# Where layer 0 adds its output bias: VectorE on the residual, or GpSimd on the gathered x

## The chip, the cores and the metric

The kernel runs on one core of one Trainium2 chip. The metric is the device time of one execution in microseconds (us), the median of several runs. One further execution was recorded by the hardware profiler; all lines of a profile come from that one.

## The reference, cut to what matters

Two transformer layers over a graph of 2708 tokens of width 512, 8 heads of 64. A token attends only to its neighbours. The layers have the same form:

```
q, k, v  = h @ Wq.T + bq,  h @ Wk.T + bk,  h @ Wv.T + bv
scores   = q . k / 8, and -1e9 where adj and the diagonal are both 0
ctx      = softmax(scores) @ v
h1 = layer_norm(h + ctx @ Wo.T + bo) * ln1_g + ln1_b
h2 = layer_norm(h1 + relu(h1 @ W1.T + b1) @ W2.T + b2) * ln2_g + ln2_b
```

In layer 0, `h` is the input `x`. The sum `h + ctx @ Wo.T + bo` is what the change touches: three terms, added in one order or in another. Everything is float32.

## The kernel before, in words

**Order of the tokens.** The kernel first finds the neighbours of every token and sorts the tokens by how many they have. Rank by rank they fall into 22 tiles of 128 tokens (the last has 20). A token's row of `x` is therefore fetched by an indirect DMA with the indices `ident_i`; this is the `gather` helper, line 982, which GpSimd issues. Keys and values of the neighbours (`kv`) come the same way, one gather for each neighbour slot of a tile.

**Attention, a step at a time.** `attend` is a generator. One step takes up to two neighbour slots of a tile: VectorE multiplies `kv` by `q` (L1019) and reduces (L1025), ScalarE takes the exponentials `p` (L1038) and weighs half of the values (L1045), VectorE weighs the other half (L1051) and adds them up in `acc` (L1058). When a tile is through, ScalarE divides (`cx`, L1089). There are five `kv` buffers, and a gather into one waits until `acc` has been added from it.

**Blocks.** The dense work goes in 11 blocks of two tiles. For each block, `attended` turns `cx` with TensorE (`tp`, L1128), gathers the tile's rows of `x` into `xb` (layer 0), and yields; then, tile by tile, it projects with Wo (`o`, L569), adds `xb` (`h`, L1254), in layer 0 adds the bias row `bo` (L1256), and normalises. `norm` is six instructions: statistics (L1112), their aggregate (L1114), `va` (L1116) on VectorE, then `rd`, a power on GpSimd (L1118), and two multiply-adds on VectorE (L1119 beside `rd`, L1122 after it). `turned` flips `h` with TensorE into `hT` (L1128, L1133). `feed_forward` then runs 16 steps `f` of eight matmuls `pf` (L1296), one ScalarE `ft` (L1304) and matmuls into `a` (L1284), and at its end adds `a` and `h` (L1316) and normalises again.

**Staging.** In the 16 steps of block k, `attended` of block k+1 starts at f = 10 and its projections come at f = 11 (one step later for k = 0). Between the steps, `advance` runs attention steps for coming tiles, paced by a credit.

**Who sets the order.** TensorE, ScalarE and the SP queue run in the order in which the program is written. VectorE and GpSimd are ordered by the compiler's planner, except inside `manual_schedule`: during the first stage and the first queries GpSimd runs as written, during the first queries VectorE too, and GpSimd runs as written through block 0 of layer 0 (`in_order`). That covers `attended` of blocks 0 and 1. From block 1's own steps on, the planner places GpSimd's instructions. An `xb` buffer comes from a ring of three (tag `row`); the planner issues the gather into it as soon as it is free.

Of the kernel before, what the change touches and what calls it, by code (L numbers as in the profile page):

```python
# [13 lines left out]
ALU = mybir.AluOpType  # L14
# [457 lines left out]
def by_edges(ctx: ExitStack, tc: tile.TileContext, x, xT, adj, layers, out, good):  # L472
# [9 lines left out]
    nc = tc.nc  # L482
# [82 lines left out]
    def project(xs, r, wm, name, other=False):  # L565

        o = (ps_f if other else ps).tile([P, DM], F32, tag="f" if other else "g", name=name)
        for c in range(NC):
            nc.tensor.matmul(o[:r], xs(c), wm[:, c, :], start=(c == 0), stop=(c == NC - 1))  # L569
        return o  # L570
# [10 lines left out]
    def size(g):  # L581
        return min(P, N - g * P)
# [390 lines left out]
    def fetch(n, to, table, g):  # L973

        r = size(g)
        if n == 0:
            gather(to[:r], table, ident_i[:r, g : g + 1])
        else:
            nc.sync.dma_start(out=to[:r], in_=table[g * P : g * P + r, :])
# [129 lines left out]
    def norm(z, r, gain, shift):  # L1109

        st = small.tile([P, 6], F32, tag="st", name="st")
        nc.vector.bn_stats(st[:r], z[:r])  # L1112
        mv = small.tile([P, 2], F32, tag="mv", name="mv")
        nc.vector.bn_aggr(mv[:r], st[:r])  # L1114
        va = small.tile([P, 1], F32, tag="va", name="va")
        nc.vector.tensor_scalar(va[:r], mv[:r, 1:2], EPS, None, ALU.add)  # L1116
        rd = small.tile([P, 1], F32, tag="rd", name="rd")
        nc.gpsimd.tensor_tensor(rd[:r], va[:r], mhalf[:r], ALU.pow)  # L1118
        nc.vector.scalar_tensor_tensor(  # L1119
            z[:r], z[:r], mv[:r, 0:1], gain[:r], ALU.subtract, ALU.mult  # L1120
        )
        nc.vector.scalar_tensor_tensor(z[:r], z[:r], rd[:r], shift[:r], ALU.mult, ALU.add)  # L1122

    def flip(z, r, to, shift=None):

        tp = ps.tile([P, NC, P], F32, tag="g", name="tp")
        for c in range(NC):
            nc.tensor.transpose(tp[:, c, :r], z[:r, c * P : (c + 1) * P], ident[:r, :r])  # L1128
        if shift is None:
            nc.scalar.copy(to, tp[:, :, :r])  # L1130
            return
        for c in range(NC):
            nc.scalar.activation(  # L1133
                to[:, c, :], tp[:, c, :r], AF.Identity, bias=shift[:, c : c + 1]
            )

    class Layer:
# [101 lines left out]
        def attended(self, block, got):  # L1239

            cTs, hs = [], []
            for g in block:
                r = size(g)
                cx = got.pop(g)
                cT = dn.tile([P, NC, P], F32, tag="cT", name="cT", bufs=3)
                flip(cx, r, cT[:, :, :r], self.bv)
                xb = dn.tile([P, DM], F32, tag="row", name="xb", bufs=3)
                fetch(self.n, xb, x if self.n == 0 else xb_d[self.n], g)
                cTs.append((g, r, cT, xb))
            yield  # L1250
            for g, r, cT, xb in cTs:
                o = project(lambda c: cT[:, c, :r], r, self.wo, "o")
                h = dn.tile([P, DM], F32, tag="h", name="h", bufs=4)
                nc.vector.tensor_tensor(h[:r], o[:r], xb[:r], ALU.add)  # L1254
                if self.n == 0:
                    nc.vector.tensor_tensor(h[:r], h[:r], self.bo[:r], ALU.add)  # L1256
                norm(h, r, self.g1, self.e1b2)
                hs.append(h)
                yield
            yield hs  # L1260
# [383 lines left out]
```

## Time and profile before

| what | value |
|---|---|
| median of 3 runs | 1964.92 us (1962.63 to 1966.28) |
| profiled execution, its own time | 1964.63 us |
| its span, first to last instruction | 1962.9 us |
| TensorE busy | 1901.0 us |
| VectorE busy | 1300.8 us |
| ScalarE busy | 933.8 us |
| GpSimd busy | 796.8 us |
| mean granted TensorE clock | 0.989 |

In the lines of the profile PE is TensorE's matmuls, PEld its weight loads, DVE VectorE, ACT ScalarE, POOL GpSimd and SP SyncE. L12 is line 12 of the kernel. A group or a line is written as output<-inputs by the program's names. A wait line gives who waited for whom, the total in us, how many times and the longest; a timeline line gives start, duration, engine, line and operation, and in brackets the idle time just before it and what ended it.

### The profile page before, as it was taken

The page shows a single profiled execution, that of the slowest core. Times are in us where ns is not written, and L with a number is a line of the kernel's source. Part 1 is how long each engine was busy: PE and PEld are TensorE (multiplying, and loading weights), DVE is VectorE, ACT ScalarE, POOL GpSimd, SP SyncE. Part 2 cuts the span into 40 slices and gives each one's busy share as a digit, 9 for nine tenths or more (in the row PEclk, how much of TensorE's full clock was granted, in tenths as well). Part 3 has the DMA queues.
Part 4 walks back from the last instruction along what each step waited for, and adds up shares of the span by engine and source line. Part 5 has one row for each costly group of instructions (what it writes and reads, how often), then busy time and mean ns, then how long its engine had stood idle before and what let it go on. Part 6 is the DMA issues. An engine that isn't in the chain of part 4 may idle for free. (4 is left out here: it accounts for less than half of the span.)

```text
span 1962.9 us, 20872 instructions
## 1 busy us (share of the span) xinstructions
PE 1901.0 (97%) x6162; PEld 1100.6 (56%) x6162; DVE 1300.8 (66%) x2142; ACT 933.8 (48%) x3219; POOL 796.8 (41%) x710
## 2 busy tenths in 40 slices
PE   8999988999999999999999998999999999999997
PEld 4444444565565655566556643556666566666664
DVE  5884587685867869659442036888688988877421
ACT  4660254564555655547332112756456765755410
POOL 3114635453555535425310022555347655644210
PEclk9999999999999999999999999999999999999998
DMA  9998766455655556546310646856455766554000
GB/s 327 352 311 307 258 211 235 161 166 189 202 161 199 188 186 227 161 150 204 130 43 27 230 162 215 298 174 217 153 177 198 247 214 209 186 190 154 34 11 13
DMA packets 131486, 366.92 MB, mean 187 GB/s; under 512 B 16668, under 2 KB 36988, under 8 KB 128654
## 3 DMA queue, kind: packets, MB, share of 16 engines
q0 software_dynamic: 69120, 246.35, 37.9%
q1 hardware_dynamic: 53332, 99.66, 14.9%
q10 hardware_dynamic: 8910, 19.48, 2.6%
q8 instruction: 50, 0.82, 0.2%
q14 instruction: 74, 0.61, 0.1%
HBM read 314.62 MB, written 50.83 MB: 186 GB/s over the span
## 5 line engine op out<-in xcount | busy, mean ns | idle before, releaser
L982 POOL DMA_INDIRECT kv<-kv_d,idx x420 | 546.1, 1300 | 475.9 <-DVE acc L1058 319.1
L1284 PE MATMUL a<-w,ft 128*128 128x512 f32 (+1 forms) x1408 | 669.9, 601 | 10.8 <-ACT ft L1304 9.5
L1296 PE MATMUL pf<-hT,w 128*128 128x256 f32 (+1 forms) x2816 | 636.3, 373 | 13.2 <-ACT ft L1304 8.8
L1296 PEld LDWEIGHTS pf<-hT,w 128*128 128x128 f32 x2816 | 521.1, 191 | 192.2 <-issue 107.3
L1284 PEld LDWEIGHTS a<-w,ft 128*128 128x128 f32 (+1 forms) x1408 | 256.5, 187 | 239.0 <-issue 201.4
L1304 ACT ACTIVATE ft<-pf,b 128x256 f32<-128x256 f32 (+1 forms) x352 | 158.5, 459 | 424.8 <-PE pf L1296 424.5
L1019 DVE TENSOR_TENSOR kv<-kv,q 128x1024 f32<-128x1024 f32 (+3 forms) x222 | 256.5, 1158 | 156.3 <-DMA kv<-kv_d,idx 103.7
L1045 ACT ACTIVATE kv<-kv,p 128x64 f32<-128x64 f32 x1232 | 311.0, 335 | 5.0
L1025 DVE TENSOR_REDUCE sc<-kv 128x16 f32<-128x1024 f32 (+3 forms) x222 | 255.2, 1154 | 1.4
L1058 DVE TENSOR_TENSOR acc<-acc,kv 128x1024 f32<-128x1024 f32 (+2 forms) x178 | 204.0, 1146 | 26.7 <-ACT kv L1045 25.9
L1118 POOL TENSOR_TENSOR rd<-va,mhalf 128x1 f32<-128x1 f32 (+1 forms) x88 | 85.4, 971 | 267.6 <-DVE va L1116 266.2
L1038 ACT ACTIVATE p<-sc,minus 128x8 f32<-128x8 f32 (+1 forms) x420 | 103.4, 295 | 161.1 <-DVE sc L1025 154.6
L569 PE MATMUL o<-wo,cT 128*128 128x512 f32 (+1 forms) x352 | 157.8, 601 | 3.7 <-DVE qs L1226 3.3
L1051 DVE TENSOR_TENSOR kv<-kv,p 128x512 f32<-128x512 f32 (+1 forms) x178 | 121.6, 684 | 52.8 <-ACT p L1038 52.7
L569 PEld LDWEIGHTS o<-wo,cT 128*128 128x128 f32 (+1 forms) x352 | 65.5, 187 | 92.2 <-issue 80.9
L1089 ACT ACTIVATE cx<-acc,su 128x64 f32<-128x64 f32 (+1 forms) x352 | 88.4, 333 | 42.6 <-DVE su L1081 33.9
L1316 DVE TENSOR_TENSOR h<-a,h 128x512 f32<-128x512 f32 (+1 forms) x44 | 29.7, 677 | 106.8 <-PE a L1284 106.7
L1122 DVE SCALAR_TENSOR_TENSOR h<-h,rd,ln_b 128x512 f32<-128x512 f32 (+1 forms) x88 | 65.9, 749 | 50.9 <-POOL rd L1118 50.9
L663 ACT ACTIVATE code<-aj 128x2708 bf16<-128x2708 int32 (+1 forms) x22 | 73.2, 3329 | 49.1 <-POOL aj L659 45.4
L1355 POOL DMA_INDIRECT kv_d<-kvs,ident_i x22 | 23.7, 1077 | 179.0 <-ACT kvs L1349 110.9
L666 DVE MAX8 tops<-code 128x8 f32<-128x247 f32 (+2 forms) x242 | 83.1, 400 | 19.3 <-ACT code L663 19.3
L1045 ACT ACTIVATE acc<-kv,p 128x64 f32<-128x64 f32 (+1 forms) x352 | 88.8, 334 | 1.4
(133 smaller groups left out, 1514.2 us busy)
## 6 DMA issues: line engine op xcount, KB each, us to landing
aj<-in_adj SPq DMA_DIRECT2D x21, 1354.0 KB, 8.0
kv_d<-kvs ACTq DMA_DIRECT2D x21, 512.0 KB, 5.6
w<-in_W SPq DMA_DIRECT2D x20, 512.0 KB, 4.8
xg<-in_xT SPq DMA_DIRECT2D x19, 512.0 KB, 8.8
kv<-kv_d,idx POOLq DMA_INDIRECT x420, 5.6
w<-in_W ACTq DMA_DIRECT2D x12, 512.0 KB, 8.9
q_d<-qs SPq DMA_DIRECT2D x22, 256.0 KB, 4.2
zT_d<-zT SPq DMA_DIRECT2D x22, 256.0 KB, 5.3
```

What stands on the lines that cost most here:

```text
L569: nc.tensor.matmul(o[:r], xs(c), wm[:, c, :], start=(c == 0), stop=(c == NC - 1))
L982: nc.gpsimd.indirect_dma_start(out=to, out_offset=None, in_=table[:, :], in_offset=bass.IndirectOffsetOnAxis(ap=s, axis=0), bounds_check=N ...
L1019: nc.vector.tensor_tensor(kv[:r, :c, :DM], kv[:r, :c, :DM], self.q[:r].unsqueeze(1).to_broadcast([r, c, DM]), ALU.mult,)
L1025: nc.vector.tensor_reduce(self.sc[:r, s0 : s0 + c, :], kv[:r, :c, :DM].rearrange("p s (h d) -> p s h d", d=DK), AX.X, ALU.add,)
L1038: nc.scalar.activation(p[:r, s, :], self.sc[:r, s, :], AF.Exp, bias=minus[:r, g, s : s + 1])
L1045: nc.scalar.activation(to[:, i, hd], kv[:r, i, DM + h * DK : DM + (h + 1) * DK], AF.Copy, scale=p[:r, s0 + i, h : h + 1],)
L1051: nc.vector.tensor_tensor(to[:, 0, :].rearrange("p (h d) -> p h d", d=DK), kv[:r, 0, DM:].rearrange("p (h d) -> p h d", d=DK), p[:r, s0, : ...
L1058: nc.vector.tensor_tensor(self.acc[:r, :c, :], self.acc[:r, :c, :], kv[:r, :c, DM:], ALU.add)
L1089: nc.scalar.activation(cx[:r, hd], self.acc[:r, 0, hd], AF.Copy, scale=self.su[:r, h : h + 1])
L1284: nc.tensor.matmul(a[:r], fts[f][:, c0 : c0 + r], self.w2[f // 2][:, f % 2, :], start=(f == 0), stop=(f == NFC - 1),)
L1296: nc.tensor.matmul(pf[:, :w], self.w1[f // 2][:, c, f % 2 * P : f % 2 * P + P], hT[:, c, :w], start=(c == 0), stop=(c == NC - 1),)
L1304: nc.scalar.activation(ft[:, :w], pf[:, :w], AF.Relu, bias=self.b1[:, f : f + 1])
```

## The change

In layer 0, the bias row `bo` is added to the gathered `xb` by GpSimd, for both tiles of the block after the `yield`, ahead of the projections. The addition to `h` on VectorE goes. Layer 1 has no such addition and stays as written.

```diff
             yield
+            if self.n == 0:
+                for g, r, cT, xb in cTs:
+                    nc.gpsimd.tensor_tensor(xb[:r], xb[:r], self.bo[:r], ALU.add)
             for g, r, cT, xb in cTs:
                 o = project(lambda c: cT[:, c, :r], r, self.wo, "o")
                 h = dn.tile([P, DM], F32, tag="h", name="h", bufs=4)
                 nc.vector.tensor_tensor(h[:r], o[:r], xb[:r], ALU.add)
-                if self.n == 0:
-                    nc.vector.tensor_tensor(h[:r], h[:r], self.bo[:r], ALU.add)
                 norm(h, r, self.g1, self.e1b2)
```

## The prediction

> **What bounds the kernel now.** I read the page's busy times first.
>
> ```profile
> PE 1901.0 (97%) x6162; PEld 1100.6 (56%) x6162; DVE 1300.8 (66%) x2142; ACT 933.8 (48%) x3219; POOL 796.8 (41%) x710
> ```
>
> TensorE leaves 1962.9 - 1901.0 = 62 us. No edit on VectorE or GpSimd can gain more than the part of those idle times that it shortens, and it loses where it adds to them. Next I asked who makes TensorE wait in layer 0's dense part (264 to 1060 us): some 20 us in all, most of it in three places. These lines are from TensorE's waits in 264 to 300, 300 to 345 and 625 to 665 us:
>
> ```profile
> PE pf L1296 <- ACT ft L1304: 7.6, 3, 3.5
> ...
> PE tp L1128 <- DVE h L1122: 3.9, 1, 3.9
> ...
> PE tp L1128 <- ACT cx L1089: 3.8, 1, 3.8
> ```
>
> Only the second is a wait for the chain that the change shortens: block 1's `h` (329.26 to 333.12 us). The other two are attention that comes late. A wait costs more than itself; busy times by stretch show the clock (10 us each, PEclk is the third number from the end):
>
> ```profile
> 329.00:339.00 10.00, 6.14 (x14) 1.61 (x12) 6.54 (x12) 2.81 (x11) 6.91 (x6) 0.66 0.49 148
> 339.00:349.00 10.00, 10.00 (x40) 7.50 (x41) 8.71 (x16) 4.21 (x17) 4.70 (x5) 1.00 0.65 232
> ```
>
> 0.66 is 6.8 us at half clock and 3.2 us at full. The half clock overlaps the wait itself, so what it takes from matmuls is some 2.5 us. The same 0.66 stands at 274 to 284 and at 632 to 642 us.
>
> **What the Trainium skill says.** "TensorE: Matmul & The Clock Gate", Part 1: an idle window of about 3.4 us halves the clock, which comes back after about as much work. The trace agrees: waits of 2.8 to 3.9 us were each followed by the half clock, waits up to 2.3 us in layer 0's later blocks by none. "SBUF — State Buffer", SBUF: two separate sides: GpSimd shares a port pair with VectorE, as an exclusive lock; a VectorE instruction with two SBUF inputs and a GpSimd instruction that reads SBUF do not overlap. The trace fits: `rd`, one column on GpSimd, takes 0.58 us at the least and 2.06 us at the most, long where VectorE runs such instructions (1.60 us at 330.68). Price of the new add: "GPSIMD Engine Reference", Elementwise, gives about 2.6 cycles an element at 1.2 GHz, so my estimate for 512 elements is 1.1 us and start-up. The nearest row:
>
> ```profile
> L659 POOL TENSOR_TENSOR aj<-aj,diag 128x128 int32<-128x128 int32 (+1 forms) x22 | 9.7, 442 | 78.6 <-DMA aj<-in_adj 74.7 <-ACT kvs L863 3.8
> ```
>
> Four times its 0.44 us is 1.8 us. I take 1.2 us, with 1.1 and 1.8 as ends, and up to 1.2 us more behind a VectorE instruction that holds the ports (L1058 runs 1.2 us).
>
> **The change, part by part.**
>
> Removed from VectorE, by the query for this line:
>
> ```profile
> L1256 DVE TENSOR_TENSOR h<-h,bo x22: 678/686/693, 256.3 to 1050.6; 128x512 f32<-128x512 f32 x21, 20x512 f32<-20x512 f32 x1
> ```
>
> 22 x 0.686 = 15.1 us busy; back to back they start 0.6 to 0.7 us apart, so about 14 us of time. Against it the lock: 22 adds x 1.2 us = 26 us in which VectorE's two-input instructions wait. At about half the time in such instructions that takes back some 13 us. VectorE as a whole gains nothing (between -14 and +12 us), under a TensorE that is the bound.
>
> Added to GpSimd: 22 adds, 26 us of 1963, no DMA. The 22 `xb` gathers stay. The wait for their landing (2.9 to 6.7 us after issue, median 4.5) moves from VectorE's `h` to GpSimd's add; queued behind that add are the gathers of `kv` and `q`, `rd`, and the writes of `kv_d`. VectorE's `h` now waits for GpSimd. What that does depends on the block.
>
> *Block 0*, all in written order. GpSimd's timeline:
>
> ```profile
> 245.31 0.99 POOL L982 DMA_INDIRECT kv<-kv_d,idx  x1 [0.30 <-issue]
> 258.19 1.02 POOL L1118 TENSOR_TENSOR rd<-va,mhalf 20x1 f32<-20x1 f32 x1 [11.89 <-DVE va L1116]
> ```
>
> Both adds fit into the 11.89 us of idle time: `xb` was issued by 240.5 and has landed by 246, the adds end by about 249 us, and `h` starts at 255.62. VectorE's norm chain up to 264.24 loses 2 x 0.71 = 1.4 us. TensorE does not wait for it (its own queries last until 263.9), but the attention behind it on VectorE does start 1.4 us sooner, and that feeds the 7.6 us of waits for `ft`. ScalarE stands between: `p` at 267.33 is written behind an `ft` that TensorE releases at 266.82, so it gains only 0.2 to 0.3 us there unless the planner reorders. I take -0.4 us, ends -1.4 and 0.
>
> *Block 1*, GpSimd still in written order, VectorE by the planner. By the program the adds (f = 12) stand behind the attention steps that f = 11 paid for, four `kv` gathers, and ahead of `rd`:
>
> ```profile
> 305.40 1.00 POOL L982 DMA_INDIRECT xb<-in_x,ident_i  x1 [0.31 <-issue]
> 306.71 1.96 POOL L982 DMA_INDIRECT xb<-in_x,ident_i  x1 [0.30 <-issue]
> 308.97 1.00 POOL L982 DMA_INDIRECT kv<-kv_d,idx  x1 [0.30 <-issue]
> 310.27 1.00 POOL L982 DMA_INDIRECT kv<-kv_d,idx  x1 [0.30 <-issue]
> ...
> 321.61 1.20 POOL L982 DMA_INDIRECT kv<-kv_d,idx  x1 [9.80 <-DVE acc L1058]
> 323.11 1.42 POOL L982 DMA_INDIRECT kv<-kv_d,idx  x1 [0.30 <-issue]
> ```
>
> The last two wait for a buffer, so the adds run from 324.6 to about 327.0, although `xb` was there at 312. VectorE, before:
>
> ```profile
> 321.85 0.68 DVE L1254 TENSOR_TENSOR h<-o,xb 128x512 f32<-128x512 f32 x1
> ...
> 325.98 0.68 DVE L1254 TENSOR_TENSOR h<-o,xb 128x512 f32<-128x512 f32 x1
> ...
> 332.31 0.75 DVE L1122 SCALAR_TENSOR_TENSOR h<-h,rd,ln_b 128x512 f32<-128x512 f32 x1 [0.46 <-POOL rd L1118]
> ```
>
> The first `h` moves from 321.85 to 325.9, the second from 325.98 to between 327.1 and 328.2. From there statistics, `rd` and the two multiply-adds take some 4.7 us by their rows, with 0 to 2 us of attention between: the end falls at 332.9 to 334.9 instead of 333.06. TensorE waits for exactly this: -0.2 to +1.8 us. I take +0.8; the half clock is paid already.
>
> *Blocks 2 to 10*, GpSimd by the planner. It issues `xb` at least 70 us ahead of `h` (489.43 for 562.09, 975.94 for 1049.85), so an add may lie anywhere between, and GpSimd has gaps: 319 us of waits for `acc` over the run. I book GpSimd's 18 x 1.2 = 22 us at nothing under these. Without that cover a `kv` gather comes up to 1.2 us later, or up to 6 us if the add stands straight behind its `xb` gather and waits for the landing. On the other side `h` comes 0.6 to 1.3 us sooner a tile, but TensorE waits for it only 0.4 us twice. Net 0, ends -2 and +8.
>
> Sum: -0.4 + 0.8 + 0 = +0.4 us on the profiled 1964.63, so **1965.0 us**; the median of the runs is 0.3 us above that execution, well inside their spread. Faster or slower by 0.2% (3.9 us) is about what a measurement of this kernel can tell from no change.
>
> **The rivals.**
>
> *Attention gets ahead (faster, 0.19).* VectorE's 1.4 us in block 0 and 1.2 us a block before 632 us reach the late attention. The waits at 274.85 (2.81 us) and 632.15 us (3.75 us) shrink below what trips the clock: about 1.2 us + 2.5 us for one, so -4 to -5 us: 1960. For it: VectorE is 9.84 of 10 us busy at 274 to 284. Against it: ScalarE's written order, and the lock.
>
> *Block 1's adds come too late (slower, 0.20).* If the adds need 2 us each under the lock, or the planner's `xb` gather of 324.83 stays ahead of them, the second add ends after 329 us and the second `h` follows. TensorE's wait then grows from 3.86 to about 7 us, and the half clock holds one 3.4 us window longer (+1.7): +5, so 1970. It decides once the second add ends after about 329 us. For it: L1118 was stretched to 1.60 us in this very place. Against it: VectorE has work to fill the hole.
>
> *The planner's new order costs a stall (slower, 0.17).* Adds that stand behind an unlanded `xb` hold up `kv` gathers; attention of the heavy tiles at 560 to 640 us has no slack, as the 3.8 us there show. One more such wait is 3.8 + 2.5 to 3.4 = about 7 us, two are 14: 1972 to 1979. Layer 1 can be reordered as well, since the planner orders VectorE and GpSimd there. Against it: 70 us of room for each add.
>
> That the removal does nothing for VectorE, since the lock gives the time back, is inside the forecast (0.44).
>
> **How the numbers follow.** Forecast 0.44 with 1962 to 1968; the others as above. Leaving out about 1 in 10 on each side (the best of the fast case, two stalls or more) gives 1959 to 1976. Faster 0.19, same 0.44, slower 0.20 + 0.17 = 0.37.
>
> **What would show it.** Right: L1256 gone, 22 new GpSimd rows of 1.1 to 1.8 us, `h` of block 0 unmoved in start, the first `h` of block 1 some 4 us later, TensorE's wait there 3.7 to 5.7 us, its busy time unchanged. Wrong: new waits of TensorE for `cx` or `ft` after 345 us, the half clock in new places, or the wait at 274.85 gone.

## Result: slower by half a per cent

The changed kernel took 1975.02 us in the median of 17 runs (1968.38 to 1979.44), the kernel before 1964.62 us in 17 runs beside it. The ratio is 1.0051, with a 95% interval of 1.0042 to 1.0060: some 10 us slower. The profiled execution of the changed kernel took 1975.02 us, with a span of 1973.3 us. It has three lines more up to the adds, so L1253 is the new add, L1257 the sum `h`, L1297 `pf`, L1305 `ft` and L1348 `kvs`.

Busy times of the changed kernel:

```profile
PE 1902.4 (96%) x6162; PEld 1102.5 (56%) x6162; DVE 1303.2 (66%) x2120; ACT 934.0 (47%) x3219; POOL 818.2 (41%) x732
```

TensorE does the same work and idles 9 us longer (1973.3 - 1902.4 = 71 us). VectorE has 22 instructions fewer, worth 15.1 us, and is still busy for 2.4 us more. So 17.5 us were added to what remains. The costliest groups of VectorE, changed kernel, say where (busy us, mean ns):

```profile
L1019 DVE TENSOR_TENSOR kv<-kv,q 128x1024 f32<-128x1024 f32 (+3 forms) x222 | 262.5, 1184 | 172.7 <-DMA kv<-kv_d,idx 117.8 <-ACT cT L1133 44.5 <-issue 7.0
L1025 DVE TENSOR_REDUCE sc<-kv 128x16 f32<-128x1024 f32 (+3 forms) x222 | 254.9, 1153 | 1.4
L1058 DVE TENSOR_TENSOR acc<-acc,kv 128x1024 f32<-128x1024 f32 (+2 forms) x178 | 209.7, 1178 | 26.5 <-ACT kv L1045 25.4
L1122 DVE SCALAR_TENSOR_TENSOR h<-h,rd,ln_b 128x512 f32<-128x512 f32 (+1 forms) x88 | 67.8, 770 | 46.9 <-POOL rd L1118 46.9
```

The same groups before:

```profile
L1019 DVE TENSOR_TENSOR kv<-kv,q 128x1024 f32<-128x1024 f32 (+3 forms) x222 | 256.5, 1158 | 156.3 <-DMA kv<-kv_d,idx 103.7 <-ACT cT L1133 43.9 <-issue 5.2
...
L1058 DVE TENSOR_TENSOR acc<-acc,kv 128x1024 f32<-128x1024 f32 (+2 forms) x178 | 204.0, 1146 | 26.7 <-ACT kv L1045 25.9
L1122 DVE SCALAR_TENSOR_TENSOR h<-h,rd,ln_b 128x512 f32<-128x512 f32 (+1 forms) x88 | 65.9, 749 | 50.9 <-POOL rd L1118 50.9
```

The reduction L1025, which reads one tensor, kept its time (1154 ns before). The three that read two tensors grew by 6.0, 5.7 and 1.9 us in all. A mean hides the form of it: the medians hardly moved, while the longest L1019 went from 1.26 to 3.97 us, L1058 from 1.25 to 3.43, L1122 from 0.79 to 2.96. Ten instructions were hit, between 329 and 928 us, each for 1.1 to 2.8 us, some 16 us together (nine in these three groups, one in the sum of `acc`, L1066).

The new add, by the query for its line (ns least, median, most):

```profile
L1253 POOL TENSOR_TENSOR xb<-xb,bo x22: 1260/1281/2237, 247.1 to 996.6; 128x512 f32<-128x512 f32 x21, 20x512 f32<-20x512 f32 x1
...
  DMA xb<-in_x,ident_i: 5.7, 3
...
  DVE h L1257: 2.7, 2
```

1.28 us at the median; GpSimd waited three times for `xb` to land, 5.7 us together, and VectorE's `h` twice for GpSimd. TensorE's waits of the changed kernel, asked for in 264 to 300, in 300 to 345 and in 625 to 680 us, in that order:

```profile
PE pf L1297 <- ACT ft L1305: 7.1, 4, 4.8
...
PE tp L1128 <- DVE h L1122: 4.7, 1, 4.7
...
PE tp L1128 <- DVE h L1122: 5.0, 1, 5.0
PE tp L1128 <- ACT cx L1089: 3.8, 1, 3.8
```

The first and the last are close to those of before. The wait for `h` in block 1 has grown from 3.9 to 4.7 us, and block 5 has a new one of 5.0 us. Busy times by stretch of the changed kernel (PEclk is the third number from the end) show what follows such waits:

```profile
329.00:339.00 10.00, 5.31 (x13) 1.80 (x14) 7.11 (x8) 2.29 (x8) 8.90 (x7) 0.66 0.26 72
...
379.00:389.00 10.00, 8.87 (x18) 4.57 (x19) 2.37 (x4) 2.03 (x8) 2.12 (x2) 0.66 0.04 8
676.00:686.00 10.00, 8.75 (x17) 4.22 (x18) 10.00 (x13) 4.56 (x18) 5.83 (x5) 0.66 0.47 142
768.00:778.00 10.00, 10.00 (x36) 7.79 (x35) 9.56 (x17) 6.75 (x26) 6.49 (x7) 0.83 0.69 258
```

The half clock of 329 us stood there before. Those of 379, 676 and 768 us are new against the kernel before. The first two also come in kernels that add nothing on GpSimd (at 383 us without any bias, at 384 and 674 us with the addition on VectorE, e1 and e2 below); that of 768 us does not.

To place the 10 us I cut each profiled execution where a block's first `tp` from `cx` starts on TensorE. Columns two and three are before and after; the others belong to experiments below.

| stage, us | before | after | no bias at all | bias on VectorE, new place | memset in place of the add | bias by DMA |
|---|---|---|---|---|---|---|
| start of block 0 | 245.2 | 246.0 | 252.9 | 251.2 | 250.4 | 246.4 |
| block 0 | 63.6 | 61.5 | 63.6 | 62.7 | 62.7 | 62.9 |
| block 1 | 81.4 | 89.6 | 84.1 | 84.5 | 83.1 | 78.6 |
| block 2 | 81.7 | 83.6 | 81.8 | 82.4 | 82.7 | 82.9 |
| blocks 3 and 4 | 159.6 | 159.3 | 157.5 | 157.5 | 157.5 | 159.0 |
| block 5 | 87.7 | 93.2 | 87.2 | 90.2 | 92.8 | 93.5 |
| block 6 | 80.8 | 83.6 | 80.1 | 80.0 | 80.6 | 79.7 |
| blocks 7 to 9 | 237.5 | 235.2 | 235.1 | 234.9 | 234.9 | 235.2 |
| block 10, to layer 1's dense part | 168.2 | 168.3 | 168.9 | 168.3 | 168.3 | 169.0 |
| from there to the end | 757.1 | 753.0 | 754.9 | 756.1 | 754.7 | 753.8 |

Before to after: block 0 gains 2.1 us, blocks 1, 2, 5 and 6 lose 8.2 + 1.9 + 5.5 + 2.8 = 18.4, and from block 7 on some 6 us come back. A single execution is a rough ruler: the start of block 0, ahead of any edit, varies by 8 us, and the profiled executions without bias (1967.9 us) and with memsets (1969.65 us) ran 6 and 7 us above the medians of their kernels. So the table is used for places, and the ratios for sizes.

**Block 1, the largest loss.** Timeline of GpSimd, changed kernel:

```profile
321.89 2.50 POOL L1253 TENSOR_TENSOR xb<-xb,bo 128x512 f32<-128x512 f32 x2
...
327.11 1.00 POOL L1118 TENSOR_TENSOR rd<-va,mhalf 128x1 f32<-128x1 f32 x1 [0.24 <-DVE va L1116]
328.96 3.98 POOL L1253 TENSOR_TENSOR xb<-xb,bo 128x512 f32<-128x512 f32 x2 [0.85 <-DMA xb<-in_x,ident_i]
332.91 0.55 POOL L1118 TENSOR_TENSOR rd<-va,mhalf 128x1 f32<-128x1 f32 x1
```

and of VectorE beside it:

```profile
328.82 0.15 DVE L1116 TENSOR_SCALAR va<-mv 128x1 f32<-128x1 f32 x1
328.88 0.74 DVE L1119 SCALAR_TENSOR_TENSOR h<-h,mv,ln_g 128x512 f32<-128x512 f32 x1
329.54 2.28 DVE L1058 TENSOR_TENSOR acc<-acc,kv 128x1024 f32<-128x1024 f32 x1
333.49 0.75 DVE L1122 SCALAR_TENSOR_TENSOR h<-h,rd,ln_b 128x512 f32<-128x512 f32 x1 [1.67 <-POOL rd L1118]
```

Block 1's own adds, at 321.89, do no harm (e6). The planner put block 2's adds, which nobody needs for another 70 us, ahead of block 1's second `rd`. The order as written ends with block 0, and it does not keep later instructions out: before the change, too, block 2's first gather of `xb` (324.83 us) runs ahead of both `rd` of block 1. `va` was ready at 329; `rd` started at 332.91. The adds first waited 0.85 us for their gather, then took 3.98 us instead of 2.5 because VectorE's `acc` ran against them, and `acc` took 2.28 us, about twice its time before. The second `h` was ready at 334.2, 1.1 us later than before, in a stage that had begun 1.3 us earlier.

TensorE's waits for the two `h` explain only a part of the stage's 8.2 us: 4.7 + 1.5 us instead of 3.9. The rest comes 45 us later. TensorE waits until VectorE has written `kvs`, the keys for layer 1, and the half clock of 379 us follows. The first line is the changed kernel's, the second that of the kernel without bias (e1), the third that of the addition on VectorE (e2), all in 345 to 420 us; the kernel before has no such wait there:

```profile
PE v L569 <- DVE kvs L1348: 2.9, 1, 2.9
...
PE v L569 <- DVE kvs L1345: 3.5, 1, 3.5
...
PE v L569 <- DVE kvs L1348: 3.8, 1, 3.8
```

Since e1 and e2 have this wait and the half clock behind it, an add on GpSimd is not needed for them. What brings them on was not tried.

**Block 5.** Timeline of GpSimd and then of VectorE, changed kernel:

```profile
672.60 1.00 POOL L982 DMA_INDIRECT kv<-kv_d,idx  x1 [0.30 <-issue]
673.61 0.59 POOL L1118 TENSOR_TENSOR rd<-va,mhalf 128x1 f32<-128x1 f32 x1
674.16 2.48 POOL L1253 TENSOR_TENSOR xb<-xb,bo 128x512 f32<-128x512 f32 x2
```

```profile
674.24 2.96 DVE L1122 SCALAR_TENSOR_TENSOR h<-h,rd,ln_b 128x512 f32<-128x512 f32 x1 [2.81 <-POOL rd L1118]
```

`rd` is late because the planner pulled the gathers ahead of it. Then `h` starts 0.08 us after the adds and needs 2.96 us instead of 0.75, with TensorE waiting for it. The table shows that this stage is long in other kernels too, with memsets and with the bias by DMA, where nothing is stretched. So the collision is plain to see here, but most of the stage's loss has another cause (e5 below).

**Block 6** shows what one collision does. Timeline of GpSimd and then of VectorE, changed kernel, and TensorE's wait in 735 to 800 us:

```profile
759.78 2.49 POOL L1253 TENSOR_TENSOR xb<-xb,bo 128x512 f32<-128x512 f32 x2
```

```profile
759.92 2.91 DVE L1066 TENSOR_TENSOR acc<-acc 128x512 f32<-128x512 f32 x1
```

```profile
PE pf L1297 <- ACT hT L1133: 3.3, 1, 3.3
```

The sum of `acc` ends a tile's attention. Behind it come `su` on VectorE, `cx` on ScalarE and, next in ScalarE's written order, `hT`, for which TensorE waits. The half clock of 768 us follows.

### The profile page after: what moved, and what is told of

It is laid out like the page before. It is cut to its first block, busy times and chain, and to the rows that moved or that the text cites. A ratio compares the mean times of both kernels' runs of the same rounds, so it can differ in the third digit from the quotient of the medians.

```text
span 1973.3 us, 20864 instructions
## 1 busy us (share of the span) xinstructions
PE 1902.4 (96%) x6162; PEld 1102.5 (56%) x6162; DVE 1303.2 (66%) x2120; ACT 934.0 (47%) x3219; POOL 818.2 (41%) x732
## 5 line engine op out<-in xcount | busy, mean ns | idle before, releaser
L982 POOL DMA_INDIRECT kv<-kv_d,idx x420 | 539.1, 1284 | 472.6 <-DVE acc L1058 320.2
L1297 PE MATMUL pf<-hT,w 128*128 128x256 f32 (+1 forms) x2816 | 637.2, 373 | 12.0 <-ACT ft L1305 7.3
L1297 PEld LDWEIGHTS pf<-hT,w 128*128 128x128 f32 x2816 | 521.7, 191 | 191.3 <-issue 107.0
L1019 DVE TENSOR_TENSOR kv<-kv,q 128x1024 f32<-128x1024 f32 (+3 forms) x222 | 262.5, 1184 | 172.7 <-DMA kv<-kv_d,idx 117.8
L1305 ACT ACTIVATE ft<-pf,b 128x256 f32<-128x256 f32 (+1 forms) x352 | 158.6, 459 | 433.6 <-PE pf L1297 433.3
L1025 DVE TENSOR_REDUCE sc<-kv 128x16 f32<-128x1024 f32 (+3 forms) x222 | 254.9, 1153 | 1.4
L1058 DVE TENSOR_TENSOR acc<-acc,kv 128x1024 f32<-128x1024 f32 (+2 forms) x178 | 209.7, 1178 | 26.5 <-ACT kv L1045 25.4
L1122 DVE SCALAR_TENSOR_TENSOR h<-h,rd,ln_b 128x512 f32<-128x512 f32 (+1 forms) x88 | 67.8, 770 | 46.9 <-POOL rd L1118 46.9
L666 DVE MAX8 tops<-code 128x8 f32<-128x247 f32 (+2 forms) x242 | 83.1, 401 | 20.0 <-ACT code L663 20.0
```

The costliest lines, as they stand in the source:

```text
L982: nc.gpsimd.indirect_dma_start(out=to, out_offset=None, in_=table[:, :], in_offset=bass.IndirectOffsetOnAxis(ap=s, axis=0), bounds_check=N ...
L1019: nc.vector.tensor_tensor(kv[:r, :c, :DM], kv[:r, :c, :DM], self.q[:r].unsqueeze(1).to_broadcast([r, c, DM]), ALU.mult,)
L1025: nc.vector.tensor_reduce(self.sc[:r, s0 : s0 + c, :], kv[:r, :c, :DM].rearrange("p s (h d) -> p s h d", d=DK), AX.X, ALU.add,)
L1058: nc.vector.tensor_tensor(self.acc[:r, :c, :], self.acc[:r, :c, :], kv[:r, :c, DM:], ALU.add)
L1297: nc.tensor.matmul(pf[:, :w], self.w1[f // 2][:, c, f % 2 * P : f % 2 * P + P], hT[:, c, :w], start=(c == 0), stop=(c == NC - 1),)
L1305: nc.scalar.activation(ft[:, :w], pf[:, :w], AF.Relu, bias=self.b1[:, f : f + 1])
```

## The experiments

Two theories stood at the start. **A**: the adds on GpSimd cost, through the ports that they share with VectorE, or through GpSimd's queue. **B**: the adds are innocent; moving the addition changes what the planner sees, and its new order happens to be worse. All ratios are to the kernel before, run on the same chip.

| kernel | ratio, 95% interval | VectorE busy, us | mean ns of L1019, L1058, L1122 |
|---|---|---|---|
| before | 1 | 1300.8 | 1158, 1146, 749 |
| after | 1.0051 (1.0042 to 1.0060) | 1303.2 | 1184, 1178, 770 |
| e1 no bias at all | 0.9957 (0.9941 to 0.9973) | 1286.9 | 1158, 1146, 746 |
| e2 same place, on VectorE | 0.9998 (0.9986 to 1.0011) | 1299.2 | 1159, 1146, 746 |
| e3 both additions | 1.0154 (1.0132 to 1.0176) | 1319.1 | 1188, 1161, 760 |
| e4 GpSimd in block 0 | 0.9994 (0.9984 to 1.0004) | 1299.9 | 1159, 1146, 748 |
| e5 memsets | 0.9979 (0.9969 to 0.9989) | 1287.1 | 1158, 1145, 746 |
| e6 GpSimd in blocks 0, 1 | 0.9998 (0.9986 to 1.0011) | 1299.1 | 1158, 1146, 748 |
| e7 GpSimd in blocks 2 to 10 | 1.0041 (1.0026 to 1.0056) | 1305.6 | 1184, 1167, 771 |
| e8 bias by TensorE | 1.0124 (1.0103 to 1.0146) | 1289.2 | 1159, 1146, 747 |
| e9 add that nobody waits for | 1.0036 (1.0025 to 1.0048) | 1296.5 | 1163, 1150, 771 |
| e10 add by add | 1.0059 (1.0039 to 1.0078) | 1303.2 | 1184, 1166, 787 |
| e11 bias by DMA | 0.9941 (0.9922 to 0.9961) | 1286.6 | 1159, 1145, 746 |
| e12 one input | 1.0015 (1.0003 to 1.0027) | 1293.1 | 1174, 1151, 751 |

### e1: no bias at all

From the kernel before:

```diff
-                if self.n == 0:
-                    nc.vector.tensor_tensor(h[:r], h[:r], self.bo[:r], ALU.add)
```

> The bias addition is left out in both places (h is only o + xb; bo is zero in these inputs, so the outputs stay the same). Theory A (the 22 GpSimd adds cost the time, by the shared ports and by holding up gathers): without them and without the VectorE adds the kernel is at least as fast as before, 1955 to 1965 us. Theory B (taking the 22 VectorE instructions out gives the planner another order, and this order is what loses): it stays slower than before, about 1970 to 1977 us.

Ratio 0.9957, so the removal alone is worth 0.43%, about 8.5 us of 1965 (5 to 12 by the interval). VectorE's means are those of before.

### e2: the same place in the program, on VectorE

From the changed kernel:

```diff
-                    nc.gpsimd.tensor_tensor(xb[:r], xb[:r], self.bo[:r], ALU.add)
+                    nc.vector.tensor_tensor(xb[:r], xb[:r], self.bo[:r], ALU.add)
```

> The new addition to xb is kept, at its new place in the program, but on VectorE. Theory A (GpSimd is the cause): back to before, 1962 to 1967 us, since VectorE has the same 22 additions as before. Theory B (order): another order again, so anything between 1960 and 1977 us; if it is the place of the addition in the program that matters, near the changed kernel's 1975.

0.9998: no change. The planner's order is a different one in this kernel as well, and `xb` is touched at the same early point; in sum neither costs anything. By stages it is not nothing: blocks 1 and 5 are longer than before (84.5 against 81.4 us, 90.2 against 87.7), and blocks 3, 4 and 7 to 9 are shorter by about as much. Theory B falls, as far as it says that any reordering costs; that the planner's order moves single stages by some us stands.

### e3: both additions

The changed kernel's adds, and VectorE's addition to `h` kept:

> VectorE keeps its addition to h, and GpSimd adds the bias to xb as well (the bias counts twice; it is zero here). VectorE has then as many instructions as before. Theory A: the whole loss and a little more, since the 1.4 us gained in block 0 go too: 1975 to 1980 us. Theory B: VectorE's list is as before, so most of the loss goes: 1964 to 1970 us.

1.0154. The 22 adds on GpSimd cost some 30 us when nothing is removed for them. From e1 to after they cost 1.0051 - 0.9957 = 0.0094, about 18.5 us. That fits a VectorE with less slack left, but the run doesn't prove that reason.

### e4: GpSimd in block 0 alone

From the kernel before:

```diff
+            early = self.n == 0 and block == blocks[0]
+            if early:
+                for g, r, cT, xb in cTs:
+                    nc.gpsimd.tensor_tensor(xb[:r], xb[:r], self.bo[:r], ALU.add)
...
-                if self.n == 0:
+                if self.n == 0 and not early:
```

> GpSimd adds the bias for block 0 alone, where both engines run in the written order and GpSimd has 11.9 us of idle time; blocks 1 to 10 add it on VectorE as before. Theory A: keeps the gain that the changed kernel's trace shows up to block 1 (TensorE reaches block 1's first cx flip 1.35 us sooner, 2.1 us sooner counted from block 0's h flip) and none of the loss: 1961 to 1964 us. Theory B: the shift alone reorders what comes after, so a gain in block 0 and a gain or loss of up to 10 us behind it.

0.9994, no change by its interval. In its profile the stage of block 0 is 1.9 us shorter (61.7 against 63.6), as in the changed kernel; what that is worth at the end is too little to be measured.

### e5: memsets in place of the add

From the changed kernel; `xb` is zero after the memsets, so layer 0's residual lacks `x` and the bias:

```diff
-                    nc.gpsimd.tensor_tensor(xb[:r], xb[:r], self.bo[:r], ALU.add)
+                    for _ in range(2):
+                        nc.gpsimd.memset(xb[:r], 0.0)
```

> In place of each of the 22 GpSimd adds stand two GpSimd memsets of the same xb (128x512 each); xb is zero after them, so layer 0's residual lacks x and the bias. A memset of that shape took 0.54 us in the trace of the kernel before, so two hold GpSimd's queue for some 1.1 us (the add: 1.28 us at the median). Kept from the change: GpSimd waits for the gather of xb to land, the gathers behind it wait too, h waits for GpSimd, VectorE's 22 adds are gone. Gone: GpSimd reads two tiles in SBUF. Theory 'ports' (the add stretches VectorE's two-input instructions): L1019, L1058 and L1122 stay at the means of the run without the addition (1158, 1146, 746 ns, not 1184, 1178, 770) and the ratio to the kernel before is 0.995 to 0.999. Theory 'queue' (what hurts is the waiting and the time in GpSimd's queue): ratio 1.003 to 1.007, as for the changed kernel, with VectorE's means unstretched. In between, 0.999 to 1.003: both.

This is the run that parts the two halves of theory A. GpSimd still waits for the gathers of `xb`, is busy with the memsets for 22.2 us (the adds: 30.8) and `h` waits for it, but it reads nothing. VectorE's groups in this kernel:

```profile
L1019 DVE TENSOR_TENSOR kv<-kv,q 128x1024 f32<-128x1024 f32 (+3 forms) x222 | 256.8, 1158 | 175.9 <-DMA kv<-kv_d,idx 119.2 <-ACT cT L1133 43.8 <-issue 9.5
...
L1058 DVE TENSOR_TENSOR acc<-acc,kv 128x1024 f32<-128x1024 f32 (+2 forms) x178 | 203.9, 1145 | 25.6 <-ACT kv L1045 24.7
```

Not a single one is stretched, and the ratio is 0.9979. So of the 0.0094, queue and waits make 0.9979 - 0.9957 = 0.0022 (some 4 us, with an uncertainty of as much), and the reading makes 1.0051 - 0.9979 = 0.0072 (some 14 us, give or take 3), together with what differs besides: the adds' 9 us more on GpSimd, and the planner's order where it isn't the same.

In two places the order is the same. In block 6 the memset kernel has the same row of VectorE's instructions; its sum of `acc` runs beside two memsets (755.95 to 756.96 us). VectorE's timeline and TensorE's wait in 735 to 800 us:

```profile
756.14 0.68 DVE L1066 TENSOR_TENSOR acc<-acc 128x512 f32<-128x512 f32 x1
```

```profile
PE pf L1298 <- ACT hT L1133: 1.6, 1, 1.6
```

0.68 us instead of 2.91, a wait of 1.6 us instead of 3.3, no half clock behind it, and a stage of 80.6 us instead of 83.6. That half clock, at 765 to 772 us, comes in every kernel in which GpSimd reads `xb` in blocks 2 to 10 (after, e3, e7, e10, e12) and in none of the others. Here one collision of 2.2 us went with 3.0 us of the stage (e7 and e10 have 83.5 and 83.6 us). Not every collision costs: two more, at 847 and 925 us, fall into blocks 7 to 9, which take 235.2 us with the adds and 234.9 with memsets.

Block 5 is the other place. GpSimd's timeline of the memset kernel, then VectorE's:

```profile
669.64 1.00 POOL L982 DMA_INDIRECT kv<-kv_d,idx  x1 [0.30 <-issue]
670.66 0.58 POOL L1118 TENSOR_TENSOR rd<-va,mhalf 128x1 f32<-128x1 f32 x1
671.19 1.93 POOL L1254 MEMSET xb<- 128x512 f32 x4
```

```profile
671.27 0.75 DVE L1122 SCALAR_TENSOR_TENSOR h<-h,rd,ln_b 128x512 f32<-128x512 f32 x1 [2.81 <-POOL rd L1118]
```

The same 2.81 us of waiting for `rd`, the same start 0.08 us after GpSimd's instruction; but 0.75 us instead of 2.96. TensorE waits 2.9 us here instead of 5.0. With no bias at all it waits 0.7 us for `h` here, with the addition on VectorE (e2) 3.8 us. So 2.9 us of this wait are there without a reading, and 2.1 came with it. The stage as a whole hardly shows those 2.1 us: 92.8 us with memsets, 93.2 with the adds.

### e6 and e7: which blocks

From the kernel before; e7 has `block not in blocks[:2]`:

```diff
+            gp = self.n == 0 and block in blocks[:2]
+            if gp:
+                for g, r, cT, xb in cTs:
+                    nc.gpsimd.tensor_tensor(xb[:r], xb[:r], self.bo[:r], ALU.add)
...
-                if self.n == 0:
+                if self.n == 0 and not gp:
```

> GpSimd adds the bias in blocks 0 and 1 only (4 of 22 adds); blocks 2 to 10 keep VectorE's add to h as in the kernel before. Theory 'the middle blocks pay' (blocks 2 to 10 lose, by stretched attention): ratio 0.997 to 1.000, the start of block 2's stage no later than 390 us plus what block 1 loses. Theory 'block 1 pays' (its two adds and the lock in the tight start): ratio 1.002 to 1.004, most of it between the starts of blocks 1 and 2.

> The other part: GpSimd adds the bias in blocks 2 to 10 (18 of 22 adds), blocks 0 and 1 keep VectorE's add to h. Theory 'the middle blocks pay': ratio 1.004 to 1.007, with waits on attention (cx, ft or h) in the stages of blocks 2 to 6. Theory 'block 1 pays': 0.999 to 1.002, and the stages of blocks 2 to 10 within 1 us each of the kernel before.

0.9998 and 1.0041. The blocks whose order is still largely written by hand cost nothing; the 18 adds of blocks 2 to 10 carry the loss. With blocks 0 and 1 left as before, TensorE waits twice for `h`: 6.0 us in block 1, where block 2's adds again stand ahead of the second `rd`, and 5.9 us in block 5 (waits in 264 to 1060 us, e7):

```profile
PE tp L1128 <- DVE h L1122: 11.8, 2, 6.0
```

### e8: bias by TensorE

From the kernel before; only the new matmul is shown, and VectorE's addition goes as in e1:

```diff
+        if add is not None:
+            nc.tensor.matmul(o[:r], ones[:1, :r], add[:1], start=True, stop=False)
```

> The bias is added by TensorE: one more matmul per tile of layer 0's output projection, a row of ones by bo (K = 1, 128x512), accumulated ahead of the four others; no VectorE add and no GpSimd add. Removing VectorE's adds gave a ratio of 0.9957 (-8.5 us); a matmul of that shape has a mean of 0.594 us in the trace of before, 22 make 13.1 us on the engine that is the bound. If they lie wholly on the path: ratio 0.9957 + 0.0067 = 1.002. If half of them fall into waits of TensorE: 0.999. A version better than both kernels only if under 0.998.

1.0124, far worse than expected. The row by the query for the line:

```profile
L569 PE MATMUL o<-bo,ones x44: 587/595/692, 254.8 to 1073.2; 1*128 1x512 f32 x42, 1*20 1x512 f32 x2
```

22 matmuls leave 44 rows of 0.595 us: a float32 matmul is two rows in these profiles, so one costs 1.19 us, and here one row of weights takes as long as 128 (0.592 us at the median in the other projections of this kernel). That is 26 us where 13.1 were expected, of some 33 us between e1 and this kernel (1.0124 - 0.9957). In the undisturbed blocks 7 to 9 each stage is 2.5 us longer than without bias (80.8 against 78.3), two matmuls' worth.

### e9: an add that nobody waits for

From the kernel without bias (e1):

```diff
+            if self.n == 0:
+                for g, r, cT, xb in cTs:
+                    nc.gpsimd.tensor_tensor(self.bo[:r], self.bo[:r], self.bo[:r], ALU.add)
```

> The bias is left out of h and of xb (as in the run without the addition, ratio 0.9957); in the place of each GpSimd add stands one that adds bo to itself, in bo's own tile: the same shape, the same two SBUF reads, but it waits for no gather, and no h waits for it. Theory 'ports': its reads are enough. L1019 and L1058 rise from 1158 and 1146 ns towards 1184 and 1178, single instructions of theirs run to over 3 us, and the ratio is 0.9957 + 0.0072 (changed kernel less memset kernel: 1.0051 - 0.9979) = 1.003, from 1.001 to 1.005. Theory 'waits' (the add costs because it waits for the gather and h waits for it): VectorE's means may rise, but the ratio stays at 0.995 to 0.999.

1.0036, in the band of the port theory, but not for its reason alone. With nothing to wait for, the planner ran the adds early and in a heap. GpSimd's timeline of this kernel:

```profile
356.65 12.68 POOL L1253 TENSOR_TENSOR bo<-bo 128x512 f32<-128x512 f32 x9
369.29 0.55 POOL L1118 TENSOR_TENSOR rd<-va,mhalf 128x1 f32<-128x1 f32 x1
```

Nine adds stood ahead of one `rd`, and block 1's stage alone took 96.4 us. The L1019 mean rose to 1163 ns, not towards 1184, and its longest instruction took 2.3 us, not over 3. The run shows that such adds hurt without any wait of their own; it does not part ports from queue.

### e10: add by add

From the changed kernel:

```diff
-            if self.n == 0:
-                for g, r, cT, xb in cTs:
-                    nc.gpsimd.tensor_tensor(xb[:r], xb[:r], self.bo[:r], ALU.add)
             for g, r, cT, xb in cTs:
+                if self.n == 0:
+                    nc.gpsimd.tensor_tensor(xb[:r], xb[:r], self.bo[:r], ALU.add)
```

> The changed kernel with each add issued right before its own tile's projection, so that the block's second add stands behind the first tile's norm and its rd on GpSimd instead of ahead of it. Same adds, same reads. Theory 'ports': VectorE's means stay at about 1184, 1178 and 770 ns, ratio 1.003 to 1.007. Theory 'order in GpSimd's queue' (the pair ahead of rd and of the kv gathers is what hurts): 0.998 to 1.002 with the same means.

1.0059, the same as the changed kernel within the intervals, with much the same stretch of VectorE. In most blocks the planner paired the adds again (at 505.84 us two stand back to back, 2.50 us for both), so the program's order was not what ran there. Writing the adds in another place does not help.

### e11: bias by DMA

From the kernel without bias (e1); only the two transfers are shown. The prefill is a broadcast row from DRAM, and the gather adds onto it:

```diff
+            if base is not None:
+                nc.sync.dma_start(out=to[:r], in_=base.to_broadcast([P, DM])[:r])
-            gather(to[:r], table, ident_i[:r, g : g + 1])
+            gather(to[:r], table, ident_i[:r, g : g + 1], base is not None)
...
             oob_is_err=False,
+            **(dict(compute_op=ALU.add) if add else {}),
```

> No engine adds the bias: SyncE's queue writes bo (from DRAM, broadcast to all rows) into xb, and the gather of x is made an accumulating one, so that xb = bo + x when it lands. Against the run without the addition (0.9957) it adds 22 transfers of 256 KB and a wait of GpSimd's gather for the first to land (transfers of that size landed 3.9 to 5.3 us after issue in the kernel before). If GpSimd has the room for that wait, as for its other waits: 0.996 to 0.999, better than both kernels. If the wait holds up the kv gathers queued behind it: 22 waits of up to 5 us, half of them on the path of attention, ratio 1.005 to 1.02. VectorE's means stay at 1158, 1146 and 746 ns in both cases.

0.9941 (0.9922 to 0.9961): faster than both kernels, as fast as without the addition within the intervals. 1959.06 us stands against 1966.69 for the kernel before on the same chip. The Trainium skill, "DMA: Bandwidth & Descriptors", section "SWDGE vs HWDGE vs iDMA", says that an accumulating transfer has to be issued by GpSimd; these gathers already are. The group of these gathers:

```profile
L984 POOL DMA_INDIRECT xb<-in_x,ident_i x22 | 35.8, 1629 | 75.2 <-DMA xb<-in_bo 60.1 <-issue 13.9 <-DVE sc L1028 0.6
```

The issue takes 1.63 us instead of 1.34, and GpSimd waits 60 us for the prefills, ten times as long as the changed kernel's GpSimd waited for its gathers. Waiting as such was not what hurt. Block 5 still has a long stage (93.5 us), so something is left to gain there.

### e12: one input

From the changed kernel; the bias is left out of the sum:

```diff
-                    nc.gpsimd.tensor_tensor(xb[:r], xb[:r], self.bo[:r], ALU.add)
+                    nc.gpsimd.tensor_scalar(xb[:r], xb[:r], 0.0, None, ALU.add)
```

> The changed kernel with the bias left out of the residual: GpSimd adds the constant 0 to xb (tensor_scalar, one SBUF input instead of two), at the same place, with the same wait for the gather and the same wait of h for GpSimd. Theory 'any SBUF read by GpSimd holds the ports, for as long as it runs': the instruction is shorter than the add's 1.26 us (say 0.6 to 1.0 us), VectorE's two-input means rise by half to three quarters of what the add did (L1019 to 1170-1178, L1058 to 1160-1170 ns), and the ratio lies between memset's 0.998 and the add's 1.005, at 1.000 to 1.003. Theory 'only a second SBUF input of GpSimd collides': means unstretched (1158, 1146, 746) and a ratio as for memset, 0.996 to 0.999.

1.0015 and stretched means (L1019 1174): an instruction of GpSimd with one SBUF input collides too, so the second theory of that text falls. The expected duration was wrong. By the query for the line:

```profile
L1253 POOL TENSOR_SCALAR xb<-xb x22: 1486/1565/2619, 253.7 to 996.1; 128x512 f32<-128x512 f32 x21, 20x512 f32<-20x512 f32 x1
```

With 1.57 us it is longer than the two-input add, yet VectorE's longest L1019 is 2.10 us instead of 3.97. It occupies GpSimd for longer and takes less from VectorE (some 6 us instead of 16), and the kernel is faster than the changed one: a sign that the collision counts more than the occupancy.

## Why the prediction missed the point and held the range

The measured 1975 us lies inside 1959 to 1976, near its upper end. The point, 1965.0, missed by 10 us, and "no change" had more weight (0.44) than "slower" (0.37). That the range held is partly luck: its upper end was drawn for two stalls in GpSimd's queue, and the queue made the smaller part of the loss.

**The price of the add** was right: 1.2 us taken, 1.28 measured at the median. The Trainium skill's estimate ("GPSIMD Engine Reference", Elementwise) of 1.1 us and start-up fits this trace.

**The lock** was sized nearly right as a sum, 13 us against some 16 us in the ten stretched instructions, and so was "VectorE as a whole gains nothing" (+2.4 us busy). The step that failed is the next one: I let equal sums of VectorE's time stand for equal time at the end. The removed 15.1 us were small pieces, two a block, and were worth 8.5 us (e1). What the lock put back came as lumps of one to nearly three us, and was worth some 14 us (e5 to after). With the queue's 4 us, put at nothing in blocks 2 to 10, this makes up the measured 10 us: 14 + 4 - 8.5. That the size of the lumps makes the difference is a guess: in e12 the pieces were under 0.9 us, and they still went with some 7 us, give or take 3 (e5 to e12).

TensorE's busy share of 97% made me treat VectorE's time as covered, while in layer 0 it is not. Among the kernels without an addition on VectorE (e8 apart, which adds to TensorE itself) the time goes up with VectorE's busy time: 1287 us at 0.994 to 0.998, 1293 at 1.0015 (e12), 1297 at 1.0036 (e9), 1303 at 1.005 to 1.006 (after and e10). Before, e2, e4 and e6, where VectorE makes all or most of the additions, have 1299 to 1301 us at 0.999 to 1.000, so they lie below that row: a us that comes from a collision went with more time than a us of VectorE's own additions.

**Blocks 2 to 10, "net 0, ends -2 and +8"**: this is the term that was mis-sized. e7 measures +8 us for it (0.0041 of 1967; 5 to 11 by the interval). The cover that I named, the gaps of GpSimd while it waits for `acc`, was there for GpSimd. It was no cover for VectorE, of which ten two-input instructions were hit beside those 18 adds. I also priced the lock for the run as a whole and then not again in these blocks. Two readings behind the term were off: TensorE waits for `h` 0.4 us once in these blocks, not twice (the wait lies on the border of two windows), and its waits in layer 0's dense part add up to 25 us, not some 20.

**Block 0**: -0.4 forecast, with -1.4 as the lower end. The stage came out 2.1 us shorter in the changed kernel, beyond that end, but e4 shows no measurable gain from it. No theory was needed here.

**Block 1**: the adds were expected at 324.6 to 327.0 and the first `h` 4 us later than before. They stood behind the two `kv` gathers as expected, but these came 2.3 us sooner (319.35 instead of 321.61); so the adds ran at 321.89 to 324.39, and `h` started at 323.20, 1.35 us later. TensorE's wait, forecast at 3.7 to 5.7 us, was 4.7 and another 1.5. But its cause was not the one named. Block 2's adds stood ahead of `rd`; I had only looked at block 1's own, and had taken GpSimd's order there for the written one. e6 (blocks 0 and 1 alone: no change) confirms that block 1's own adds were harmless.

**The rivals.** "The planner's new order costs a stall" gave the right size, 1972 to 1979, and new waits after 345 us and the half clock in new places did come. They are not the waits for late attention at 560 to 640 us that it named: the one of 3.8 us there is unchanged. Its mechanism is a quarter of the truth. Held-up queues are e5's 4 us; the order alone costs nothing in sum (e2). The rest is the lock, which I had under "inside the forecast". "Block 1's adds come too late" named a place that did lose, for another reason. "Attention gets ahead" did not happen in the changed kernel. In e1 and e11 the removal did gain, and e11's 1959 is near its 1960, but not by its mechanism: the wait for `cx` that it wanted to shrink is still 3.7 and 3.8 us there, and the waits for `ft` up to 305 us are 8.8 and 9.1 us instead of 7.6. The likeness of the numbers is chance. In e1's stages the gain shows in blocks 3, 4 and 7 to 9.

**Open.** How the 8.2 us of block 1 divide between queue, order and ports was not tried on its own; e9 was meant to help and did not. In the memset kernel block 2's writes stand ahead of the second `rd` as well, and the stage takes 83.1 us; in e12 VectorE is hardly stretched in block 1 (0.3 us), and the stage takes 90.2 us. So the stretch of VectorE alone does not explain that stage. The planner's order was not held fixed between any two kernels; the 14 us can contain some of it. The parts of e1, e5 and after have intervals of 0.001 to 0.002 each, so 4 and 14 us are sizes and not exact shares.

## What to carry to other kernels

An addition moved from VectorE to GpSimd isn't off VectorE: where VectorE mostly runs two-input instructions on SBUF, GpSimd's reading comes back as VectorE's time (here 31 us of adds as some 16), in lumps, at places that the planner picks. Before a sum is booked as "hidden under the bound engine", ask whether the second engine has any slack in that stage; here a share of 66% hid stretches of 98%. If the operand comes by an indirect DMA anyway, let the DMA add: here that cost no time that could be measured, and GpSimd 0.3 us more for each gather's issue.

## What the runs showed of the hardware that was not expected

The Trainium skill, "SBUF — State Buffer", SBUF: two separate sides, says that whichever starts first gets the shared ports for its whole instruction. The traces show a harsher case for VectorE. GpSimd's and VectorE's timelines of the changed kernel:

```profile
506.44 2.50 POOL L1253 TENSOR_TENSOR xb<-xb,bo 128x512 f32<-128x512 f32 x2
```

```profile
506.06 3.97 DVE L1019 TENSOR_TENSOR kv<-kv,q 128x1024 f32<-128x1024 f32 x1
```

VectorE's instruction had started 0.38 us ahead of the adds. The two adds ran at full speed (2.50 us for both), and it took 3.97 us instead of 1.21: it waited for both, and did not get in between them. At 329 us both sides were slowed (adds 3.98 us, `acc` 2.28 us). So the first to start isn't always the one that keeps the ports, and a VectorE instruction that meets a pair of adds can pay for both.

That page's other statements hold. A GpSimd instruction that only writes does not collide (e5, no stretch in 44 memsets), and VectorE instructions with one SBUF input do not either: L1025 stayed at 1153 ns, and `h` from PSUM and `xb` (L1257) took its usual 0.69 us beside an add at 323.20.

How long a wait of TensorE may be before the half clock follows is not sharp in these traces: one of 2.3 us was followed by it (e5, 714 us), one of 2.4 us was not (e1, 442 us).
